# One core of a two-layer transformer: FP4 feed-forward products in split reduced precision, and small vector operations handed to POOL

## The chip, the cores and the metric

The program runs on one core of one Trainium2 chip. That core has a matrix engine (TensorE; PE is its matmuls and PEld its weight loads), VectorE (DVE), ScalarE (ACT), GpSimd (POOL) and a queue for transfers (SP). The metric is the device time of one execution in microseconds. Before the change it is 1334.26 us, the median of 3 runs (1334.25 to 1334.98).

## The reference

The input x has 8 sequences of 512 rows and 256 columns. Two layers follow, each of them x = x + attention(layernorm(x)), then x = x + ffn(layernorm(x)):

- Layer 0, attention: 16 heads of 16 columns, causal over all 512 positions, with gamma and beta on the normalized input and one weight for q, k and v.
- Layer 0, feed-forward: `h = silu(gate) * y`, hidden width 704, where every product is an "FP4 linear". Blocks of 16 values, of the weights and of the inputs alike (and of h), are scaled by their largest magnitude over 6 and rounded to the grid 0, 0.5, 1, 1.5, 2, 3, 4, 6. So the layer has three matrix products, and a rounding to the grid ahead of each.
- Layer 1, attention: the same heads, but a row sees only itself and the 63 before it; four weights and four biases.
- Layer 1, feed-forward: hidden width 768, weights that are integers from -127 to 127 over 127, no rounding of the inputs.

## The kernel before, in words

A sequence is one "batch" b of 8, held in SBUF as `X[b]`: 128 partitions by 4 row tiles t by 256 columns. The work goes through four stages: attention 0, FFN 0, attention 1, FFN 1.

**Attention** (function `attention`, used twice). A unit is a batch and half of the heads, a quad is four heads of a unit, so there are 32 quads per stage. Three ways of ordering matter. The PE work is written out by hand and pinned in program order (`pin`). All other instructions are put in order on their engines by a planner, which works with modelled costs; an engine then executes its own list strictly in that order. And `body` sets what is interleaved: while quad i makes its exponentials (`Outputs`), the scores of quad i+2 are formed only to find the row maxima (`scores`, whose `tensor_reduce` on DVE is L469 in attention 0 and L488 in attention 1). `maxima(i+2)` (L508) then splits each maximum into three bfloat16 pieces by two subtractions in a row on DVE, and `max_rows` (pm, L519) turns the pieces by a matmul into rows that enter the next product. It runs one quad later, at step 3 of 6 in attention 0 and at step 1 of 4 in attention 1. The exponentials come from ACT (L575, L605), POOL clears what the mask forbids (`only`, L134), and PE sums (`sums`, L635).

Beside this run the preparations for later batches. `row_stats` makes the layernorm statistics: DVE `bn_stats`, then ve (L161, L165) on DVE, the power -1/2 on POOL (rs, L166) and mr on DVE again (L168); `normalize` (L174) is on ACT. `load_q`, `load_k` and `stores` form q and k in three bfloat16 pieces (L374 to L378 on ACT and DVE, L387 and L390 on POOL), write them to HBM and fetch them back in another layout. In attention 0 a generator, `filler`, is advanced three times in ten steps: it rounds the FP4 weights (`quantize` with `exact`) and prepares the first batch of FFN 0.

**FFN 0** works on 32 tiles of 128 rows. `gated` (L1026) forms gate and up in two halves of 352 columns by 4-byte matmuls, whose records come two to a matmul. ACT takes silu (L1031) and DVE multiplies (L1032). `quantize` rounds h: a reduce (L217), the scale (L223), its reciprocal (L224), a correction of the reciprocal (L225), a product on POOL (L226), ACT (L274), two operations on DVE (L276, L278) and a product on POOL (L279). `down` transposes h on PE (L1041), copies it to SBUF in three pieces on ACT (L1045 to L1048), multiplies it by wd1 (L1052), and DVE adds it to X (L1056). It runs two tiles behind `gated`. `prepare` makes the inputs of the next batch in the same way, tagged x. Late in the stage the integer weights of layer 1 arrive and `opening` of attention 1 begins.

**FFN 1** already uses the type float32r, with a high and a low half of its inputs; one record is one matmul there (L1159, L1131).

## Time and profile before

| | |
|---|---|
| median of 3 runs | 1334.26 us |
| the profiled execution, its own time | 1330.82 us |
| its span on the core | 1329.1 us |
| mean granted TensorE clock | 0.98 |
| attention 0 with its start (0 to 486) | 486 us |
| FFN 0 (486 to 806) | 320 us |
| attention 1 (806 to 1165) | 359 us |
| FFN 1 (1165 to 1329) | 164 us |

The bounds of the stages are read from the first and last start of each line's instructions; the end of one and the beginning of the next overlap by a few us. A line of a group reads: line, engine, operation, output<-input, shapes, count | busy us, mean ns of one | idle time of the engine just before them, and who ended it. A line of a timeline reads: start, duration, engine, line, operation, count, and in brackets the idle time before it. A line of stages reads: start:end, length, then for each engine the busy us and the number of instructions, the granted clock, the share of the DMA engines and GB/s.

### The profile page before, as it was taken

The numbers are of one execution on the slowest core, as the hardware profiler recorded it, in microseconds if no ns is written. First come the engines' busy times: TensorE is split into PE (matmuls) and PEld (weight loads), VectorE is DVE, ScalarE is ACT, GpSimd is POOL, SyncE is SP. The second block draws the span as 40 slices with busy tenths as digits, with TensorE's granted clock in tenths as the row PEclk, the third lists the DMA queues.
The fourth block names the chain that finished last, engine by engine and source line by source line (L and its number), as shares of the span: only waits on it lengthen the run. The fifth ranks groups of instructions, "written<-read, shape, count | busy, mean of one in ns | idle before, by whom it ended". The sixth has DMA issues, their size and how long they took to land. (4 is left out here: it accounts for less than half of the span.)

```text
span 1329.1 us, 23108 instructions
## 1 busy us (share of the span) xinstructions
PE 1185.7 (89%) x8815; PEld 791.4 (60%) x8846; DVE 929.9 (70%) x1657; ACT 650.8 (49%) x1057; POOL 688.7 (52%) x912
## 2 busy tenths in 40 slices
PE   4678889889978998998999998999999999889998
PEld 2444454445534455665666666676767667668887
DVE  4699989796699847686766657676667767545553
ACT  3265655566665663332333323544455444555553
POOL 4266556464456334443443544766667566634443
PEclk9899999899989998999999999999999999999999
DMA  7643334354433310000000044454543535000001
GB/s 219 142 103 75 87 80 91 83 111 87 96 68 97 60 33 1 24 24 0 1 1 0 0 111 93 96 123 84 113 103 91 125 80 128 7 0 33 25 33 42
DMA packets 50448, 92.07 MB, mean 69 GB/s; under 512 B 6428, under 2 KB 43420, under 8 KB 44188
## 3 DMA queue, kind: packets, MB, share of 16 engines
q1 hardware_dynamic: 49452, 89.74, 29.6%
q8 instruction: 72, 1.18, 0.4%
q10 hardware_dynamic: 816, 0.79, 0.2%
q14 instruction: 44, 0.36, 0.1%
q0 software_dynamic: 64, 0.00, 0.0%
HBM read 61.15 MB, written 29.36 MB: 68 GB/s over the span
## 5 line engine op out<-in xcount | busy, mean ns | idle before, releaser
L134 POOL TENSOR_SCALAR_AFFINE_SELECT ex<-ex 128x256 f32<-128x256 f32 (+2 forms) x512 | 263.4, 525 | 230.3 <-ACT ex L575 129.9
L575 ACT ACTIVATE ex<-t 128x1024 f32<-128x1024 f32 (+1 forms) x192 | 168.0, 882 | 121.1 <-PE t L564 110.7
L469 DVE TENSOR_REDUCE mx<-s 128x2 f32<-128x1024 f32 (+2 forms) x192 | 196.6, 1035 | 39.9 <-PE s L458 30.6
L605 ACT ACTIVATE ex<-t 128x640 f32<-128x640 f32 (+1 forms) x128 | 96.8, 757 | 123.4 <-PE t L595 108.6
L635 PE MATMUL po<-ex,vp 128*32 128x128 f32 (+4 forms) x2816 | 142.9, 322 | 3.1 <-POOL ex L134 2.0
L488 DVE TENSOR_REDUCE mx<-s 128x4 f32<-128x768 f32 x128 | 121.3, 953 | 31.9 <-PE s L482 30.9
L1052 PE MATMUL pd<-wd,hT 128*128 128x256 f32 (+1 forms) x384 | 101.3, 407 | 15.9 <-ACT hT L1045 15.1
L635 PEld LDWEIGHTS po<-ex,vp 128*32 128x32 f32 x2816 | 71.2, 109 | 60.5 <-issue 31.2
L1103 POOL TENSOR_TENSOR hT<-gh,hT 128x512 fp32r<-128x512 f32 x48 | 61.7, 1291 | 82.6 <-ACT hT L1102 66.1
L453 PE MATMUL s<-kk_both,qq_both 96*128 96x512 bf16 (+3 forms) x352 | 81.9, 314 | 19.0 <-DVE mx L469 8.8
L1052 PEld LDWEIGHTS pd<-wd,hT 128*128 128x128 f32 (+1 forms) x384 | 70.1, 195 | 47.9 <-ACT hT L1045 28.0
L279 POOL TENSOR_TENSOR h<-mg_h,sc_h 128x704 f32<-128x704 bf16 x32 | 45.4, 1420 | 97.6 <-DVE mg_h L278 90.3
L1026 PE MATMUL gu<-wg,fyT 128*128 128x352 f32 x256 | 93.9, 470 | 0.0
L1026 PE MATMUL gu<-wu,fyT 128*128 128x352 f32 x256 | 86.3, 459 | 0.0
L475 PE MATMUL s<-wmask,ident_b 128*128 128x384 bf16 x256 | 83.6, 332 | 1.4 <-DVE mx L488 1.4
L564 PE MATMUL t<-qq_both,kk_both 108*128 108x512 bf16 (+3 forms) x352 | 70.4, 304 | 12.1 <-DVE mx L469 6.1
L226 POOL TENSOR_TENSOR xn_h<-h,rc_h 128x704 f32<-128x704 f32 x32 | 45.0, 1405 | 61.1 <-DVE rc_h L225 57.5
L458 PE MATMUL s<-cmask,ident_b 128*128 128x128 bf16 (+1 forms) x321 | 76.4, 238 | 0.0
L1170 DVE SCALAR_TENSOR_TENSOR gh<-ggu,gsl 128x512 f32<-128x512 f32 x48 | 33.2, 691 | 55.6 <-ACT gsl L1168 55.1
L1031 ACT ACTIVATE sl<-gu 128x352 f32<-128x352 f32 x64 | 29.4, 460 | 75.8 <-PE gu L1026 75.6
L1026 PEld LDWEIGHTS gu<-wu,fyT 128*128 128x128 f32 x256 | 48.6, 190 | 27.4 <-issue 1.0
L453 PEld LDWEIGHTS <-qq_both 96*128 96x128 bf16 x352 | 32.6, 101 | 51.5 <-issue 29.6
(256 smaller groups left out, 2661.1 us busy)
## 6 DMA issues: line engine op xcount, KB each, us to landing
q_hbm<-qp SPq DMA_DIRECT2D x96, 128.0 KB
k_hbm<-kp SPq DMA_DIRECT2D x96, 128.0 KB
qq_both<-q_hbm SPq DMA_DIRECT2D x44, 256.0 KB
kk_both<-k_hbm SPq DMA_DIRECT2D x22, 384.0 KB
qq_both<-q_hbm SPq DMA_DIRECT2D x44, 128.0 KB
kk_both<-k_hbm SPq DMA_DIRECT2D x22, 256.0 KB
qq<-q_hbm SPq DMA_DIRECT2D x20, 256.0 KB
out_dram<-go SPq DMA_DIRECT2D x16, 256.0 KB
```

What stands on the lines that cost most here:

```text
L134: nc.gpsimd.affine_select(out=t, in_=t, compare_op=ALU.is_ge, fill=0.0, base=base, pattern=[[0, n] for n in shape[1:-1]] + [[sign, shape[- ...
L453: pin(nc.tensor.matmul(bank[:, a * w : (a + 1) * w], lhsT=q[:KF, hs[j], t * P : w], rhs=k[:KF, hs[j], :w], start=(a == 0), stop=False, ski ...
L458: pin(nc.tensor.matmul(bank.rearrange("p (i k) -> p i k", k=w)[:, :, t * P :], lhsT=ident_b, rhs=cmask[:, : len(part), :], start=False, st ...
L469: nc.vector.tensor_reduce(dst, src, AX.X, ALU.max)
L475: pin(nc.tensor.matmul(sc[:, a, : 2 * BAND], lhsT=ident_b, rhs=mask.rearrange("p a k -> p (a k)"), start=True, stop=False,))
L488: nc.vector.tensor_reduce(mx[:, t2 : t2 + 2, js[0] : js[0] + 2].rearrange("p t j -> p j t"), sc[:, :, : 2 * BAND].rearrange("p j (t k) -> ...
L564: pin(nc.tensor.matmul(bank[:, a * w : (a + 1) * w], lhsT=k[: KF + 12, self.hs[j], t * P : (t + 1) * P], rhs=q[: KF + 12, self.hs[j], t * ...
L575: nc.scalar.activation(ex[:, :banks, :used], sc[:, :banks, :used], AF.Exp, scale=QSCALE)
L605: nc.scalar.activation(by_head[:, :, :w], sc[:, :, :w], AF.Exp, scale=QSCALE)
L635: pin(nc.tensor.matmul(self.o[HP * j : HP * (j + 1), t * P : t * P + w], lhsT=vp[:, kt, 4 * c + j, :], rhs=self.ex[kt, j][:, x0 : x0 + w], ...
L1026: nc.tensor.matmul(gu[:, i, :352], lhsT=YT[b][:, e, t * P : (t + 1) * P], rhs=w[:, e, f], start=(e == 0), stop=(e == NE - 1),)
L1052: nc.tensor.matmul(pd[:, :D], lhsT=hT[:n, k, :], rhs=wd1[:n, k, :], start=(k == 0), stop=(k == NH - 1),)
```

## The change

FFN 0: the 4-byte matmuls become three float32r matmuls each, high by high, high by low, low by high. The weights are split at the end of `filler` (wg, wu and the inputs of batch 0) and at the start of the stage (wd); every later input and h is split as it leaves PSUM (`split`: a copy on ACT, a subtraction on DVE). h is padded from 704 to 768 columns. The transposes of a tile (`turn_rows`) move ahead of `gated`, three tiles behind it, and `down` stays after it. `prepare` starts one tile earlier. `quantize` in its inexact form works in place, and its correction of the reciprocal is gone (the constant of the scale takes its place).

Attention: the two subtractions of `maxima` go from DVE to POOL. The statistics' operations after `bn_aggr` are all on POOL. Statistics are taken one quad before `normalize`, and `normalize` is spread over four steps. Masks are added by `minus_b` with the opposite sign. The second tile of values and `cmask` move into the pools of the stages, so the clearing of that tile on POOL happens at the start of each attention's body. The opening of attention 1 keeps its pieces of q and k in a shared tile and has one remainder buffer.

```diff
-        nc.vector.tensor_scalar(ve, mv[:, :, 1], EPS, None, ALU.add)
         if twice:
-            nc.vector.scalar_tensor_tensor(ve, ve, EPS, mv[:, :, 1], ALU.mult, ALU.add)
+            nc.gpsimd.tensor_scalar(ve, mv[:, :, 1], EPS, EPS, ALU.add, ALU.mult)
+            nc.gpsimd.tensor_tensor(ve, ve, mv[:, :, 1], ALU.add)
+        else:
+            nc.gpsimd.tensor_scalar(ve, mv[:, :, 1], EPS, None, ALU.add)
         nc.gpsimd.tensor_tensor(rs, ve, mhalf, ALU.pow)
         mr = small.tile([P, NT], F32, tag="mr", name=f"mr_{tag}")
-        nc.vector.scalar_tensor_tensor(mr, mv[:, :, 0], -1.0, rs, ALU.mult, ALU.mult)
+        nc.gpsimd.tensor_tensor(mr, mv[:, :, 0], rs, ALU.mult)
+        nc.gpsimd.tensor_scalar(mr, mr, -1.0, None, ALU.mult)
...
-            nc.vector.tensor_scalar(sc, am, sixth, 1e-12, ALU.mult, ALU.max)
+            nc.vector.tensor_scalar(sc, am, SIXTH_UP, 1e-12, ALU.mult, ALU.max)
             nc.vector.reciprocal(rc, sc)
-            nc.vector.tensor_scalar(rc, rc, DOWN, None, ALU.mult)
-            nc.gpsimd.tensor_tensor(blocks(xn), src, wide(rc), ALU.mult)
+            nc.gpsimd.tensor_tensor(src, src, wide(rc), ALU.mult)
...
+    PAIRS = ((0, 0), (0, 1), (1, 0))
+    def split(hi, lo, src):
+        nc.scalar.copy(hi, src)
+        nc.vector.tensor_tensor(lo, src, hi.bitcast(F32), ALU.subtract)
...
             for a in range(2):
-                nc.vector.tensor_tensor(
+                nc.gpsimd.tensor_tensor(
                     mx[:, :, a + 1, :], mx[:, :, a, :], upper(mx)[:, :, a, :], ALU.subtract
                 )
...
+            padded_values(home[0], 1, nc.gpsimd)
             norm(1)
...
+                if r == 0 and c + 2 < B:
+                    at(f3, lambda: stats(c + 2))
                 if r == 1 and c + 2 < B:
-                    at(f1, lambda: norm(c + 2))
+                    for t in range(NT):
+                        at(t, lambda t=t: norm(c + 2, [t]))
...
+        for t, nm, homes in (
+            (wg1, "wg", (high, high)), (wu1, "wu", (high, high)), (YT[0], "y", (wp, wp)),
+        ):
...
+            for e in range(NE):
+                nc.scalar.copy(hi[:, e], t[:, e])
+                nc.gpsimd.tensor_tensor(lo[:, e], t[:, e], hi[:, e].bitcast(F32), ALU.subtract)
+                yield
...
+        nc.scalar.copy(wd_halves[0], wd1)
+        nc.gpsimd.tensor_tensor(
+            wd_halves[1], wd1, wd_halves[0].bitcast(F32), ALU.subtract
+        )
...
-            for i, w in enumerate((wg1, wu1)):
+            for i, w in enumerate((HALVES["wg"], HALVES["wu"])):
+                n = 0
                 for e in range(NE):
-                    nc.tensor.matmul(
-                        gu[:, i, :352], lhsT=YT[b][:, e, t * P : (t + 1) * P],
-                        rhs=w[:, e, f], start=(e == 0), stop=(e == NE - 1),
-                    )
+                    for l, r in PAIRS:
+                        nc.tensor.matmul(
+                            gu[:, i, :352], lhsT=YT[b][l][:, e, t * P : (t + 1) * P],
+                            rhs=w[r][:, e, f], start=(n == 0), stop=(n == 3 * NE - 1),
+                        )
+                        n += 1
...
+        def turn_rows(b, t):
+            h = HID.pop((b, t))
+            hT = HT[b, t] = [
+                fp.tile([P, NH, P], F32R, tag=f"hT{i}", name=f"hT{i}_{b}_{t}", bufs=1)
+                for i in range(2)
+            ]
+            pt = psum2(f"ph_{b}_{t}").rearrange("p a k -> p (a k)")
+            for k in range(NH):
+                nc.tensor.transpose(
+                    pt[:, k * P : (k + 1) * P], h[:, k * P : (k + 1) * P], ident
+                )
+            flat = [x.rearrange("p k t -> p (k t)") for x in hT]
+            split(flat[0], flat[1], pt[:, : NH * P])
...
+            for l, r in PAIRS:
+                for k in range(NH):
+                    nc.tensor.matmul(
+                        pd[:, :D], lhsT=hT[l][:, k, :], rhs=wd_halves[r][:, k, :],
+                        start=(l == r == k == 0), stop=(l == 1 and k == NH - 1),
                     )
...
-        for n in range(len(tiles) + 2):
+        for n in range(len(tiles) + 3):
+            if n >= 3:
+                turn_rows(*tiles[n - 3])
...
-                if t == 0 and b + 1 < B:
-                    ahead = prepare(b + 1)
+                if n == 0:
+                    ahead = prepare(1)
+                    for _ in range(3):
+                        next(ahead)
+                elif t == NT - 1 and b + 2 < B:
+                    ahead = prepare(b + 2)
                 gated(b, t, 0)
                 gated(b, t, 1)
...
-            if n >= 2:
-                down(*tiles[n - 2])
+            if n >= 3:
+                down(*tiles[n - 3])
```

## The prediction

> **What bounds the kernel now.** I read the page's slices first, then the busy time of each engine by stage, then PE's timeline in the two feed-forward stages, and last the waits in the attentions. By stage:
>
> ```profile
> 66.00:300.00 234.00, 200.16 (x1507) 110.92 (x1522) 211.05 (x340) 139.92 (x197) 135.40 (x169) 0.98 0.42 90
> 300.00:366.00 66.00, 64.89 (x501) 35.44 (x505) 45.36 (x67) 43.16 (x63) 28.98 (x49) 1.00 0.43 90
> 366.00:465.00 99.00, 83.35 (x656) 45.06 (x663) 88.71 (x187) 61.25 (x86) 50.70 (x72) 0.95 0.35 75
> 529.40:761.50 232.10, 217.72 (x889) 145.55 (x887) 162.64 (x277) 83.23 (x189) 97.59 (x67) 0.99 0.03 7
> 835.00:1165.00 330.00, 306.22 (x3549) 225.12 (x3548) 222.84 (x398) 160.61 (x241) 220.37 (x387) 0.98 0.42 94
> ```
>
> The columns after the length are PE, PEld, DVE, ACT, POOL. Attention 0 is bound by DVE (211 of 234 us, 89 of 99) wherever the rounding of the weights runs beside it, and by PE (65 of 66) where it does not. FFN 0 (24 tiles here) is bound by PE: 218 of 232, with DVE at 163. Attention 1 is bound by PE with 24 us of gaps; POOL is 67% busy. FFN 1 fills PE.
>
> One FFN 0 tile on PE lasts 9.67 us (one gate-up-transposes-down round is 605.37 to 615.04 in the timeline):
>
> ```profile
> 610.27 0.76 PE L1026 MATMUL gu<-wg,fyT 128*128 128x352 f32 x2
> 612.06 3.05 PE L1052 MATMUL pd<-wd,hT 128*128 128x256 f32 x12 [1.03 <-ACT hT L1045]
> 615.04 0.86 PE L1026 MATMUL gu<-wg,fyT 128*128 128x352 f32 x2
> 616.92 1.35 PE L1026 MATMUL gu<-wg,fyT 128*128 128x352 f32 x4
> 618.10 1.35 PE L1026 MATMUL gu<-wu,fyT 128*128 128x352 f32 x4
> 619.29 0.82 PE L1041 MATMUL ph<-ident,h 128*128 128x128 f32 x6
> ```
>
> Starts count, not durations, since matmuls overlap. 616.92 to 618.10 is 1.18 us for four records, which are two 4-byte matmuls: 0.59 us each. 612.06 to 615.04 is 2.98 us for the six of `down`, with 1.03 us of waiting for ACT's copy ahead of them. FFN 1 shows what the new type costs:
>
> ```profile
> 1199.74 1.07 PE L1159 MATMUL ggu<-yT,wu_r 128*128 128x512 f32 x4
> 1200.65 1.59 PE L1131 MATMUL gpd<-wd_r,hT 128*128 128x256 f32 x12
> 1202.09 1.09 PE L1159 MATMUL ggu<-yT,wg_r 128*128 128x512 f32 x4
> ```
>
> Four of 512 columns start within 0.91 us (0.2275 each), twelve of 256 within 1.44 us (0.120 each). Between the two, 352 columns cost 0.160.
>
> **FFN 0, PE.** Removed: 8 gate and up matmuls x 0.59 = 4.72 us, `down` 2.98, the wait 1.03. Kept: six transposes 0.65 (619.29 to 619.94), two of the inputs at 0.1 each, 0.2. That is 9.58 of the 9.67. Added: 24 x 0.160 = 3.84 and 18 x 0.120 = 2.16; the wait should go, because the copies (ACT about 0.8, DVE 0.95) then lie under 3.84 us of gate and up. New PE time 3.84 + 2.16 + 0.65 + 0.2 = 6.85, with 0.35 for hand-overs 7.2 us.
>
> **FFN 0, DVE**, which is late next. The rows for 24 tiles:
>
> ```profile
> L278 DVE SCALAR_TENSOR_TENSOR mg_x<-mg_x,xn_x 128x1024 bf16<-128x1024 bf16 x6 | 10.7, 1792 | 0.0
> L225 DVE TENSOR_SCALAR rc_h<-rc_h 128x44 f32<-128x44 f32 x25 | 10.0, 398 | 0.6
> L276 DVE SCALAR_TENSOR_TENSOR xn_x<-mg_x,xn_x 128x1024 f32<-128x1024 bf16 x6 | 7.4, 1225 | 15.9 <-ACT mg_x L274 15.9
> L225 DVE TENSOR_SCALAR rc_x<-rc_x 128x64 f32<-128x64 f32 x6 | 7.0, 1165 | 0.0
> ```
>
> The correction L225 goes: 17.0 us. L278 writing 4-byte values in place should cost what L276 does: 3 us less for x, nothing for h (907 and 905 ns). Added: the low half of h, 24 times 768 columns out of PSUM. The same subtraction of 512 columns takes 685 ns (L1103), an addition of 256 takes 416 (L1056), so 0.95 us, 22.8 in all; and 12 low halves of inputs x 0.685 = 8.2. Sum 162.6 - 17.0 - 3 + 31.0 = 174 us, 7.25 us a tile against 6.78. So PE falls to 7.2 while DVE rises to 7.25: neither hides the other. Two engines that hand work to each other in fixed orders do not both reach 100%. DVE in attention 0 reaches 90%; at that share the tile takes 8.0 us. Ends: 7.3 (DVE full) and 9.0 (80%). Gain 32 x 1.67 = 53 us. ACT falls (one copy of 768, about 0.8, for three of 585, 274 and 264 ns) and POOL stays at 4.1 us a tile: both are covered at half load, and without that cover would have to double first.
>
> Splitting the weights: ACT four copies of 704 and two of 512 (about 4 us at 585 ns for 512), POOL four subtractions of 704 and two of 512 (4 x 1.39 + 2 x 1.16 = 7.9 us). They use six more steps of `filler`, about 20 of the stage's 372, and end around 465 us by where the inputs' transposes lie now (441 us). Then PE is the one that is full and DVE is at 35%: nothing. If `filler` ran past the end, up to 8 us. wd: ACT 1.5, POOL 2.7 us (1.93 for 1024, 1.5 ns per further element), needed only by the third round; POOL's products for the first tiles wait behind it: 2 us taken, 0 to 4. The transfers keep number and size; the integer weights land in wd's old place, in a stage where DMA is 3% busy. The tighter buffers of the opening make PE wait for at most a store now and then, spread over eight rounds: nothing, 3 us if uncovered. FFN 0 in all: -51 us.
>
> **Attention, the maxima.** 128 subtractions of 16 elements leave DVE. Their cost there is uneven:
>
> ```profile
> 211.84 0.17 DVE L508 TENSOR_TENSOR mx<-mx 128x16 f32<-128x16 f32 x1
> 230.72 1.12 DVE L508 TENSOR_TENSOR mx<-mx 128x16 f32<-128x16 f32 x1
> ```
>
> 0.17 us alone, 1.12 while POOL works; 24.0 us in attention 0, 16.2 in attention 1. On POOL no row shows them. A tensor_tensor there costs 728 ns for 256 elements and 1930 for 1024, so 352 for 16; the smallest mask operation (128 columns) takes 297, the power on 4 elements 1020. I take 0.35, between 0.3 and 1.0: 0.7 us per quad, 45 us in all, and POOL goes from 67% to about 75% busy in attention 1. Where the table of engine selection in the Trainium skill's GPSIMD Engine Reference (4.1) gives elementwise work to VectorE, with GpSimd about twice slower, it speaks against this; twice DVE's 325 ns would be 83 us of POOL instead of 45, still inside its gaps. The page SBUF — State Buffer ("The single rule") adds that the two engines take an exclusive port lock, so the 45 us could come back as stalls of DVE's two-input operations; by it attention 0 would gain nothing.
>
> What waits: `max_rows` on PE. In attention 1 the pieces were ready at 953.68 us and used at 957.80: 4.1 us of slack, during which POOL has casts, subtractions and masks without a gap (953.85 to 961.5). The two can stand behind one of these, 1.2 to 1.4 us, and still be in time.
>
> **Attention, the statistics.** Of 8 batches and four kinds, 3 DVE instructions (4 where `twice`) become 3 or 4 on POOL, 104 more there x 0.35 = 36 us, under 0.1 to 1.0 each. What DVE loses is not only their time but a wait, since it stands still until POOL's power is done:
>
> ```profile
> 966.54 0.17 DVE L161 TENSOR_SCALAR ve_c<-mv_c 128x4 f32<-128x4 f32 x1
> 967.85 0.16 DVE L168 SCALAR_TENSOR_TENSOR mr_c<-mv_c,rs_c 128x4 f32<-128x4 f32 x1 [1.14 <-POOL rs_c L166]
> 967.92 0.95 DVE L488 TENSOR_REDUCE mx<-s 128x4 f32<-128x768 f32 x1
> 968.79 0.74 DVE L378 SCALAR_TENSOR_TENSOR qr<-pq,qcol,qp 128x512 f32<-128x512 f32 x1
> ```
>
> ```profile
> PE pm L519 <- DVE qr L378: 12.5, 12, 1.4
> ```
>
> Behind mr_c stand a reduce and qr, and for qr's bank PE's pm waits: 12.5 us in attention 1. With the statistics a quad earlier I expect about 7 of these back, less 3 for masks that come later from a fuller POOL: -4 us (between -12 and +10).
>
> Attention 0: in the two DVE-bound stretches DVE loses some 19 us of maxima (13.8 of them in 66 to 300), some 7 of the statistics' 10.2 and 3 of waits: 29 us. PE has 49 us of gaps there. I take half, -15, because POOL's load rises from 56% to 66% and stretches what DVE keeps; ends 0 and -29. The 66 us bound by PE keep their time.
>
> **The rest**: clearing the values' tile (1.83 us on POOL) falls into 5.9 us in which POOL is idle before its first cast in attention 1, and into a POOL 23% busy at 33 to 66 us; the first statistics get a longer POOL chain (about +0.8); other signs of masks nothing; FFN 1 nothing, PE being full. Together +2.
>
> **Sum.** -51 - 4 - 15 + 2 = -68. The profiled execution took 1330.82 us (span 1329.1 and 1.7 around it), 3.4 less than the median; I set it against the median: 1334.26 - 68 = 1266.
>
> **Rivals.** *Both engines fit better*: 7.4 us a tile, 71 from FFN 0 after its start, 25 in attention 0, 8 in attention 1, the same +2: 1232. For it: three tiles of distance between h and its transposes. Against: DVE then at 98%. *DVE's order sets FFN 0*: one buffer for the transposed h means a late low half stops `down`, then the next transposes; at 9.0 us a tile 21 - 2 = 19, attention 0 gives 8, attention 1 nothing: 1309. *POOL too late for the maxima*, the slower side: the pieces stand behind masks that themselves wait for ACT (up to 3.7 us per wait). Once POOL lags by more than the slack of 4.1 us, every quad's pm waits; from 68 / 64 = 1.06 us of PE waiting per quad on, the gain is gone, at 1.5 us the time is 1334 - 68 + 96 = 1362. Against it: POOL has a third of attention 1 idle, most of it waiting for ACT, and the pieces are ready before the last mask. *The new matmuls cost twice that*: 24 x 0.32 + 18 x 0.24 + 1.2 = 13.2 us a tile, 113 us more in FFN 0, 1430 with the -17 elsewhere; FFN 1's rows speak against it, and I give it nothing.
>
> **How the numbers follow.** Forecast 45%; better fit 22%; DVE's order 18%; POOL too late 5%; 7% between forecast and DVE's order, 3% beyond the better fit. Range 1232 to 1308, from one outer case to the other. 0.2% is what a measurement here tells from no change. Faster 0.94, within 0.01, slower 0.05.
>
> **What will show it.** FFN 0: tile distance near 8.0 us, DVE about 90% busy, no L1052 wait on ACT, 24 records of 352 columns at 0.16 us. Attention 0: DVE's share down, L508's place on POOL near 0.35 us each. Attention 1: pm without waits for qr; po's waits for POOL up little. It is wrong if the subtractions take 1 us on POOL, if 352 columns cost over 0.2 us, or if PE waits in FFN 0 for the low halves.

## The result, and the profile after

The changed kernel takes 1324.74 us (1324.02 to 1325.49): a ratio of 0.9941 to the kernel before, with a 95% interval of 0.9917 to 0.9965 (the two medians alone give 0.9929). The profiled execution took 1324.02 us with a span of 1322.3. So 9.5 us came in by the medians where 68 were forecast, and the time lies above the range.

The four stages, from the first gate matmul, the last `down` matmul, the first gate matmul of FFN 1 and the end of the span (us):

| | attention 0 | FFN 0 | attention 1 | FFN 1 |
|---|---|---|---|---|
| before | 485.6 | 321.2 | 367.4 | 154.9 |
| after | 492.8 | 300.8 | 375.0 | 153.8 |
| difference | +7.2 | -20.4 | +7.6 | -1.1 |

The differences add up to 6.7 us and not to 9.5, because the profiled execution of the kernel before was 3.4 us faster than its median. FFN 0 gained less than half of what was expected, and both attentions lost. The stages of the changed kernel; columns as in the prediction: stretch, length, busy us and instructions of PE, PEld, DVE, ACT, POOL, granted clock, share of the DMA engines, GB/s.

```profile
66.00:300.00 234.00, 199.11 (x1436) 108.37 (x1450) 180.43 (x257) 131.19 (x183) 139.14 (x208) 0.92 0.38 81
300.00:366.00 66.00, 56.00 (x431) 30.98 (x432) 50.44 (x83) 40.17 (x58) 35.70 (x58) 0.92 0.50 105
366.00:465.00 99.00, 91.20 (x733) 50.76 (x741) 81.23 (x149) 72.00 (x105) 70.45 (x117) 1.00 0.35 76
493.00:793.00 300.00, 257.18 (x1657) 242.87 (x1657) 238.37 (x378) 111.08 (x189) 145.31 (x113) 0.93 0.11 28
823.00:1160.00 337.00, 310.56 (x3568) 228.16 (x3567) 207.88 (x333) 163.17 (x246) 234.90 (x466) 0.98 0.42 93
```

DVE did lose its work in attention 0: 211 us of the first 234 became 180. A part of that is work that had not been reached yet; over the whole of attention 0 DVE's busy time falls from 387.9 to 359.6 us and POOL's rises from 249.1 to 289.3. But PE is at 199 of 234 as before: no engine is near full in this stretch now, and no time was won. In FFN 0 neither PE (257 of 300) nor DVE (238) is full. And the granted clock fell from 0.98 to 0.92 in the first stretch and from 0.98 to 0.93 in FFN 0.

**Attention 0.** From the timeline of the changed kernel:

```profile
122.06 1.23 POOL L158 TENSOR_SCALAR ve_a<-mv_a 128x4 f32<-128x4 f32 x1
123.37 0.20 POOL L159 TENSOR_TENSOR ve_a<-ve_a,mv_a 128x4 f32<-128x4 f32 x1
123.65 1.05 POOL L162 TENSOR_TENSOR rs_a<-ve_a,mhalf 128x4 f32<-128x4 f32 x1
124.78 0.20 POOL L164 TENSOR_TENSOR mr_a<-mv_a,rs_a 128x4 f32<-128x4 f32 x1
125.06 0.23 POOL L165 TENSOR_SCALAR mr_a<-mr_a 128x4 f32<-128x4 f32 x1
125.33 0.60 ACT L171 ACTIVATE y<-x,mr_a,rs_a 128x256 f32<-128x256 f32 x1 [5.26 <-POOL mr_a L165]
125.83 1.00 ACT L591 ACTIVATE ex<-t 128x1024 f32<-128x1024 f32 x1
126.89 0.80 PE L580 MATMUL t<-qq,kk 108*128 108x384 bf16 x2 [5.18 <-ACT ex L591]
```

The statistics' chain on POOL begins at 122.06 and ends at 125.29; the last of `bn_aggr` was done at 120.95. ACT, whose next instruction in its list is `normalize`, stands still for 5.26 us, the exponentials stand behind it, and PE waits 5.18 us for these. From 124.2 on the clock is at one half for 6.8 us.

**Attention 1** repeats this on a smaller scale:

```profile
863.32 0.23 POOL L161 TENSOR_SCALAR ve_c<-mv_c 128x4 f32<-128x4 f32 x1
863.63 1.04 POOL L162 TENSOR_TENSOR rs_c<-ve_c,mhalf 128x4 f32<-128x4 f32 x1
865.30 0.60 ACT L171 ACTIVATE by<-x,mr_c,rs_c 128x256 f32<-128x256 f32 x1 [2.53 <-POOL mr_c L165]
865.80 0.67 ACT L393 ACTIVATE qp<-pq,qcol 128x512 bf16<-128x512 f32 x1
866.57 0.75 DVE L394 SCALAR_TENSOR_TENSOR qr<-pq,qcol,qp 128x512 f32<-128x512 f32 x1 [0.92 <-ACT qp L393]
867.38 0.38 PE L535 MATMUL pm<-minus_b,mx 128*12 128x128 bf16 x4 [1.94 <-DVE qr L394]
```

The power waits behind POOL's masks, `normalize` for the power, qp behind `normalize`, DVE's qr for qp, and PE's pm for qr's bank. Over the stage pm waits 17.4 us for qr, against 14.0 before: the wait that the forecast saw going has grown. The pieces of the maxima themselves are never late: no wait of pm for them exceeds 0.2 us. The clock adds to the wait for qr: it drops to one half at 868.3, 916.1, 963.9 and 1011.7 us, each time right after pm has waited 1.94 to 1.96 us.

**FFN 0.** A tile's pitch (first gate matmul to the next tile's) goes 6.6, 8.2, 11.1, 6.6 in batch 2, 6.6, 6.7, 11.0, 10.7 in batch 5: mean 8.80 us over tiles 4 to 28, against 9.54 before. Of these 24 tiles 9 run at PE's own time, 6.6 to 6.7 us; the others are stretched. The stage's first four tiles (30.7 us before, 31.5 after) and its last whole three (35.0 and 36.2) gained nothing. In a stretched tile:

```profile
573.95 2.32 DVE L274 SCALAR_TENSOR_TENSOR fy<-mg_x,fy 128x1024 f32<-128x1024 bf16 x1
576.41 1.93 POOL L275 TENSOR_TENSOR fy<-fy,sc_x 128x1024 f32<-128x1024 f32 x1 [1.22 <-DVE fy L274]
578.38 0.19 DVE L220 TENSOR_SCALAR sc_h<-am_h 128x44 f32<-128x44 f32 x1 [0.99 <-POOL fy L275]
578.40 0.66 PE L878 MATMUL pt_f<-ident,fy 128*128 128x128 f32 x4 [0.86 <-POOL fy L275]
579.85 1.84 POOL L222 TENSOR_TENSOR h<-h,rc_h 128x704 f32<-128x704 f32 x1 [1.50 <-DVE rc_h L221]
581.37 0.97 PE L1141 MATMUL pd<-wd_high,hT 128*128 128x256 f32 x6 [0.90 <-DVE hT L285]
583.09 0.55 PE L1130 MATMUL ph<-ident,h 128*128 128x128 f32 x3 [0.75 <-POOL h L275]
```

The next batch's inputs (fy) pass through the same engines, and PE stops three times. Its waits in the stage (total, times, longest):

```profile
PE ph L1130 <- POOL h L275: 11.6, 8, 2.5
PE pt_f L878 <- DVE fyT L285: 7.6, 4, 3.1
PE pd L1141 <- DVE hT L285: 7.5, 6, 3.0
PE pt_f L878 <- POOL fy L275: 6.8, 3, 5.0
PE pd L1141 <- ACT hT L284: 4.6, 6, 2.3
```

**The clock.** Around one wait of 2.48 us in FFN 0, by windows of 3.4 us; the granted clock is the third number from the end:

```profile
649.90:653.30 3.40, 0.92 (x9) 0.72 (x8) 2.94 (x3) 1.62 (x3) 2.04 (x2) 0.99 0.00 0
653.30:656.70 3.40, 2.78 (x13) 2.41 (x12) 3.18 (x7) 1.32 (x3) 0.82 (x1) 0.50 0.00 0
656.70:660.10 3.40, 3.40 (x14) 3.40 (x13) 1.75 (x3) 2.24 (x6) 2.37 (x2) 0.50 0.01 2
660.10:663.50 3.40, 3.40 (x28) 3.40 (x26) 2.45 (x4) 1.40 (x3) 0.00 (x0) 1.00 0.00 0
```

PE was busy for 0.92 of the first window, and two windows at half clock follow; gate matmuls start 0.29 us apart there and 0.16 apart from 660.24 on. Half of PE's busy time inside such windows is what the clock cost at most: 21.8 us in the kernel before, 51.7 after (attention 0 11.9 and 20.8, FFN 0 4.8 and 19.1, attention 1 5.1 and 10.1, FFN 1 0 and 1.7).

### The profile page after: what moved, and what is told of

It is laid out like the page before. It is cut to its first block, busy times and chain, and to the rows that moved or that the text cites. A ratio compares the mean times of both kernels' runs of the same rounds, so it can differ in the third digit from the quotient of the medians.

```text
span 1322.3 us, 24142 instructions
## 1 busy us (share of the span) xinstructions
PE 1154.8 (87%) x9263; PEld 841.9 (64%) x9294; DVE 895.7 (68%) x1462; ACT 652.6 (49%) x1000; POOL 762.5 (58%) x1158
## 3 DMA queue, kind: packets, MB, share of 16 engines
q8 instruction: 75, 1.23, 0.4%
## 5 line engine op out<-in xcount | busy, mean ns | idle before, releaser
L275 POOL TENSOR_TENSOR h<-h,sc_h 128x704 f32<-128x704 f32 x32 | 45.8, 1433 | 72.8 <-DVE h L274 72.8
L491 PE MATMUL s<-wmask,minus_b 128*128 128x384 bf16 x256 | 84.6, 336 | 2.2 <-DVE mx L504 2.2
L580 PE MATMUL t<-qq_both,kk_both 108*128 108x512 bf16 (+3 forms) x352 | 72.2, 310 | 13.1 <-DVE mx L485 6.5
L474 PE MATMUL s<-cmask,minus_b 128*128 128x128 bf16 (+1 forms) x321 | 77.8, 242 | 0.0
L222 POOL TENSOR_TENSOR h<-h,rc_h 128x704 f32<-128x704 f32 x32 | 48.5, 1516 | 50.2 <-DVE rc_h L221 41.9
L1141 PE MATMUL pd<-wd_high,hT 128*128 128x256 f32 x384 | 60.6, 296 | 12.1 <-DVE hT L285 7.5
L1111 PE MATMUL gu<-wg_wgh,fyT 128*128 128x352 f32 x224 | 69.1, 350 | 0.0
L1111 PE MATMUL gu<-wu_wuh,fyT 128*128 128x352 f32 x224 | 65.4, 334 | 0.0
L1141 PEld LDWEIGHTS pd<-wd_high,hT 128*128 128x128 f32 x384 | 53.4, 199 | 15.3 <-DVE hT L285 8.7
L1256 PE MATMUL ggu<-yT,wg_r 128*128 128x512 f32 x192 | 57.5, 412 | 1.2 <-ACT yT L1199 0.8
L498 PE MATMUL s<-kk_both,qq_both 96*128 96x128 bf16 (+1 forms) x352 | 57.0, 244 | 0.4 <-DMA kk_both<-k_hbm 0.4
```

The lines of the kernel that those rows point to most:

```text
L474: pin(nc.tensor.matmul(bank.rearrange("p (i k) -> p i k", k=w)[:, :, t * P :], lhsT=minus_b, rhs=cmask[:, : len(part), :], start=False, st ...
L491: pin(nc.tensor.matmul(sc[:, a, : 2 * BAND], lhsT=minus_b, rhs=mask.rearrange("p a k -> p (a k)"), start=True, stop=False,))
L580: pin(nc.tensor.matmul(bank[:, a * w : (a + 1) * w], lhsT=k[: KF + 12, self.hs[j], t * P : (t + 1) * P], rhs=q[: KF + 12, self.hs[j], t * ...
L1111: nc.tensor.matmul(gu[:, i, :352], lhsT=YT[b][l][:, e, t * P : (t + 1) * P], rhs=w[r][:, e, f], start=(n == 0), stop=(n == 3 * NE - 1),)
L1141: nc.tensor.matmul(pd[:, :D], lhsT=hT[l][:, k, :], rhs=wd_halves[r][:, k, :], start=(l == r == k == 0), stop=(l == 1 and k == NH - 1),)
```

## The experiments

"Stages" gives attention 0, FFN 0, attention 1. The kernel before took 1331.8 to 1334.3 us beside these runs (medians); ratios are to that. A stage is read from one profiled execution and varies more than the median of a kernel: e2, e5 and e6, which differ in FFN 0 alone, have 498.7, 492.5 and 491.1 us in attention 0, while e7, e9, e11, e15 and e16, which run one and the same order there, have 485.4 to 487.2. So a stage that differs by a few us shows little unless the whole times go with it.

### The two moves undone, one by one and together

e1, on the changed kernel:

```diff
-                nc.gpsimd.tensor_tensor(
+                nc.vector.tensor_tensor(
                     mx[:, :, a + 1, :], mx[:, :, a, :], upper(mx)[:, :, a, :], ALU.subtract
```

> The changed kernel with the two subtractions of the maxima back on DVE, all else kept. Queue theory (what POOL and ACT wait for in their queues costs the attentions more than DVE's relief gives): POOL no longer stands still for DVE's maxima (32 us in the changed kernel), time 1312 to 1320. Relief theory (as predicted, the freed DVE time is worth half of itself in attention 0): DVE gets 40 us back, 1332 to 1345.

1329.54 us, 0.997 [0.9956, 0.9985]; stages 499.4, 296.6, 374.8.

e2, on the changed kernel (e3 is e1 and e2 together):

```diff
-            nc.gpsimd.tensor_scalar(ve, mv[:, :, 1], EPS, EPS, ALU.add, ALU.mult)
-            nc.gpsimd.tensor_tensor(ve, ve, mv[:, :, 1], ALU.add)
...
+        nc.vector.tensor_scalar(ve, mv[:, :, 1], EPS, None, ALU.add)
+            nc.vector.scalar_tensor_tensor(ve, ve, EPS, mv[:, :, 1], ALU.mult, ALU.add)
...
-        nc.gpsimd.tensor_tensor(mr, mv[:, :, 0], rs, ALU.mult)
-        nc.gpsimd.tensor_scalar(mr, mr, -1.0, None, ALU.mult)
+        nc.vector.scalar_tensor_tensor(mr, mv[:, :, 0], -1.0, rs, ALU.mult, ALU.mult)
```

> The changed kernel with ve and mr of the statistics back on DVE, all else kept. Queue theory: ACT's wait for mr in attention 1 falls from 21 us to below 10, PE's wait for pm's bank from 17 to about 12, time 1314 to 1321. Relief theory: DVE waits for POOL's power again, 1328 to 1336.

1316.41 us, 0.9866 [0.985, 0.9883]; stages 498.7, 297.8, 364.8.

> Both back on DVE. Queue theory: the sum of the two, 1303 to 1316. Relief theory: 1335 to 1355. If the two moves hardly matter: within 4 us of 1324.7, and the missing gain is all in FFN 0 and in the clock.

1324.59 us, 0.9927 [0.9906, 0.9947]; stages 498.1, 300.8, 365.9.

What follows: with the statistics taken early, attention 1 is 365 to 366 us with their operations on DVE and 375 with them on POOL, wherever the maxima are: 10 us. Undone together, the two moves cancel in the whole time (1324.59 against 1324.74 us). In attention 0 undoing them brings nothing back: it is at 498 us without either move, so its loss lies elsewhere too.

### Attention 0: which part of the change costs it

e7 is e3 without early statistics and without the spread `normalize`; e11 is e3 without early statistics alone:

```diff
-                if r == 0 and c + 2 < B:
-                    at(f3, lambda: stats(c + 2))
...
-                    for t in range(NT):
-                        at(t, lambda t=t: norm(c + 2, [t]))
+                    at(f1, lambda: norm(c + 2))
```

> On e3_both_on_dve (1324.59 us, attention 0 498.1 us against 485.6 before): the statistics are no longer taken a quad early and normalize is again issued in one step. If this order of issue is what costs attention 0 its 12 us, it goes back to 486 to 489 us and the whole to 1311 to 1316 us; attention 1 then has its waits of before again, 365 to 368 us. If it is not (the rest of the change, or where the half-clock windows fall), attention 0 stays at 494 to 502 us and the whole at 1320 to 1329 us.

1310.89 us, 0.9853 [0.9815, 0.9891]; stages 487.2, 299.7, 366.6. Up to quad 24 every quad starts within 1.2 us of where it started in the kernel before, so splitting the weights costs attention 0 next to nothing, as the forecast had it.

> On e7_norm_as_before (1310.89 us, attention 0 487.2 us): normalize is spread over four steps again, but the statistics are still taken when it begins; e3_both_on_dve, with the statistics a quad early as well, had 498.1 us in attention 0. If the spreading costs the 11 us, attention 0 is at 495 to 500 us and the whole at 1318 to 1326 us; if taking the statistics early does, attention 0 is at 486 to 489 us and the whole at 1309 to 1314 us.

1311.16 us, 0.9844 [0.9818, 0.9871]; stages 487.0, 299.4, 367.2. The spreading costs nothing (the instructions of DVE, ACT and POOL come in the same order in attention 0 as in e7); taking the statistics a quad early, with their operations on DVE, costs attention 0 the 11 us.

e8 is the kernel before with the two moves alone (both edits of e1 and e2, reversed):

> The kernel before with only the two moves of the change's name: the statistics' small operations and the two subtractions of the maxima on POOL, everything else as it was (statistics taken when normalize is issued). Relief theory (half of the DVE time freed in attention 0 returns, pm's waits for qr go): 1311 to 1322 us. Queue theory (a longer chain on POOL behind masks, ACT's normalize waits for it, and gaps over half a clock window drop the clock): within 5 us of 1334.3 or slower, 1330 to 1346 us.

1342.59 us, 1.0083 [1.0054, 1.0112]; stages 498.9, 318.7, 372.2. The two moves alone make the kernel before slower by 0.8%; attention 0 is 13.3 us longer. They did not come back as slower work on DVE: of its instructions in attention 0, those that both kernels have take 1.2 us more in all, in 389 us.

e10 is e7 with the maxima on POOL:

> On e7_norm_as_before (1310.89 us; attention 0 487.2, attention 1 366.6 us): of the attention's changes only the maxima's subtractions are on POOL. Relief theory (13.8 us less on VectorE in the stretch of attention 0 that it bounds, half of it returned): attention 0 478 to 483 us, in all 1302 to 1307 us. Queue theory (what VectorE gains is lost where a maximum's pieces stand behind casts and masks on POOL, and in half-clock windows): attention 0 486 to 495 us, in all 1309 to 1319 us.

1309.01 us, 0.9826 [0.98, 0.9853]; stages 482.7, 299.0, 369.6. Against e7 the maxima on POOL gain 1.9 us in all, 4.5 in attention 0, and attention 1 is 3.0 longer.

e18 is the changed kernel without early statistics (the first two lines of the diff of e7):

> The changed kernel (1324.74 us, attention 0 492.8, attention 1 375.0 us) with the statistics taken when normalize begins, not a quad earlier; their operations and the maxima stay on POOL. If the early place is what disturbs attention 0 (11 us with the operations on VectorE): attention 0 480 to 486 us; attention 1 then waits longer for the chain on POOL, 375 to 380 us; in all 1312 to 1322 us. If the early place costs only with the operations on VectorE: attention 0 489 to 497 us, in all 1321 to 1334 us.

1323.54 us, 0.993 [0.9908, 0.9952]; stages 501.2, 301.3, 368.4. Attention 0 came out above both expectations, and attention 1 did not wait longer, against the first: only the early place and POOL together cost it its time. From e10 the kernel differs by the statistics' operations on POOL (and by the spreading, which cost nothing in e11), and attention 0 is 18.5 us longer, the whole 14.5. This pair shows best that relief is not time.

The four kernels with the maxima on POOL, whole time, then attention 0 and 1 (us):

| | statistics' operations on DVE | on POOL |
|---|---|---|
| taken with `normalize` | e10: 1309.0; 482.7, 369.6 | e18: 1323.5; 501.2, 368.4 |
| taken a quad early | e2: 1316.4; 498.7, 364.8 | changed kernel: 1324.7; 492.8, 375.0 |

Each of the two, the early place and POOL, lengthens attention 0 by itself, and they do not add up. In the changed kernel as it is, POOL's 8.3 us (against e2) lie in attention 1. To the pair of the first row: from e10, and then from e18, the stretch 66 to 465 and ACT's wait for the statistics in 60 to 480:

```profile
66.00:465.00 399.00, 351.77 (x2679) 194.43 (x2707) 329.97 (x536) 249.40 (x354) 240.83 (x356) 0.96 0.40 84
...
ACT y L168 <- DVE mr_a L162: 10.6, 5, 6.4
```

```profile
66.00:465.00 399.00, 346.44 (x2565) 188.93 (x2568) 308.34 (x483) 236.22 (x335) 235.83 (x374) 0.93 0.40 84
...
ACT y L171 <- POOL mr_a L165: 24.8, 6, 9.2
```

DVE is busy 21.6 us less in the same 399 us, but PE does fewer instructions too (2565 for 2679): over the whole of attention 0 DVE is freed of 8.6 us (368.9 and 360.3). `normalize` waits 14.2 us longer, for a chain that stands between POOL's masks and casts; and what the half clock costs PE there rises from 14.3 to 22.1 us at most. The same wait of ACT is 11.6 us in the kernel before, 23.2 in the changed one, 24.8 in e8, 22.5 in e1, 11.9 in e2, 15.0 in e3 and 11.7 in e11. Among the kernels without early statistics (before, e10, e11 against e8, e18) attention 0 is long where this wait is; among those with them it is not so: e2 has 11.9 us of it and 498.7 us, the changed kernel 23.2 and 492.8. So the wait goes with the loss only where the statistics are taken late; that it is the cause there is argued from the timeline above, and no run separates it from the planner's new order. With the statistics on POOL an earlier place helps attention 0 (501.2 to 492.8); with them on DVE it hurts (487.0 to 498.1), where this wait explains 3 us at most.

One thing that goes with the losses is a wait of DVE of 6.7 to 7.4 us for the second half of the up weights, whose transfer is issued near 235 us behind stores of k, near 200 in the kernel before. e13 and e14 issue it earlier:

```diff
+        def rounded(n, *args):
+            for i, _ in enumerate(quantize(*args)):
+                if i == 4:
+                    load(n + 1)
+                yield
...
```

> The changed kernel (1324.74 us, attention 0 492.8 us) with the transfer of the next part of the weights issued at the fifth step of the part before it, where it was issued when its own rounding begins. If the transfer's place behind the stores of k is what costs attention 0 its time (7.0 us of VectorE standing for it, and the rounding of the up weights some 50 us later than in the kernel before): no such wait, attention 0 480 to 487 us, in all 1311 to 1319 us. If the wait only goes with another cause (gaps over half a clock window): attention 0 489 to 497 us, in all 1320 to 1330 us.

1322.07 us, 0.9902 [0.9865, 0.9939]; stages 490.0, 302.4, 375.0. That wait is gone.

> The same edit on e12_own_buffers_maxima (1305.01 us, attention 0 481.0 us). If the place of the transfer is the cause: attention 0 474 to 479 us, in all 1297 to 1303 us; if not, 1303 to 1311 us.

1311.18 us, 0.9841 [0.982, 0.9863]; stages 488.3, 296.0, 366.8, slower than e12 below. So the late transfer is not the cause; e10 has that wait too (6.8 us), and is the shorter in attention 0 (482.7 us). Why the early place costs attention 0 time with the operations on DVE stays open. PE's loss to the clock there is 22.9 us at most in e3 against 13.1 in e11, which goes with the loss but was not separated from it.

### FFN 0: what stretches the tiles

e4, on the changed kernel:

```diff
-            hT = HT[b, t] = [
-                fp.tile([P, NH, P], F32R, tag=f"hT{i}", name=f"hT{i}_{b}_{t}", bufs=1)
-                for i in range(2)
-            ]
+            one = fp.tile([P, NH, P], F32R, tag="hT0", name=f"hT0_{b}_{t}", bufs=1)
+            hT = HT[b, t] = [one, one]
...
-            split(flat[0], flat[1], pt[:, : NH * P])
+            nc.scalar.copy(hT[0].rearrange("p k t -> p (k t)"), pt[:, : NH * P])
```

> The changed kernel without the low half of h: its subtraction on DVE (0.95 us a tile) is left out, and down's third product takes the high half again, so PE's work is the same. If DVE's load sets FFN 0: tiles fall by about 1 us, 25 to 32 us in all, 1293 to 1300. If the wait for the next batch's inputs and the clock that falls in its gaps set it: tiles without prepare stay at 6.6, the others lose little, 1312 to 1322.

1323.84 us, 0.9909 [0.9882, 0.9936]; FFN 0 301.5, mean tile 8.71 us. The first line is e4, the second the changed kernel:

```profile
530.00:710.00 180.00, 152.67 (x1043) 149.56 (x1042) 139.21 (x209) 68.69 (x120) 86.47 (x55) 0.95 0.03 10
```

```profile
530.00:710.00 180.00, 156.36 (x1038) 151.15 (x1038) 153.22 (x232) 70.09 (x121) 84.35 (x54) 0.93 0.03 10
```

DVE falls from 85% to 77%, and the tiles are as long as they were. So neither a late low half of h nor DVE's mean load sets the pitch. DVE's load where it is bunched is another matter. The four tiles of batch 5 in the changed kernel, and the third of these in e4:

```profile
664.20:670.80 6.60, 6.60 (x51) 6.60 (x49) 5.46 (x11) 2.39 (x4) 4.27 (x3) 1.00 0.01 4
670.80:677.50 6.70, 6.70 (x52) 6.69 (x50) 6.27 (x7) 2.70 (x5) 1.39 (x1) 1.00 0.00 0
677.50:688.50 11.00, 8.33 (x55) 7.67 (x53) 10.42 (x15) 3.45 (x6) 6.06 (x4) 0.95 0.00 0
688.50:699.20 10.70, 9.14 (x54) 8.76 (x53) 7.78 (x13) 4.96 (x9) 3.26 (x3) 0.73 0.01 2
```

```profile
684.80:695.30 10.50, 8.64 (x58) 8.40 (x57) 9.77 (x15) 3.84 (x7) 6.22 (x5) 0.90 0.00 1
```

In the first stretched tile DVE is busy for 10.42 of 11.0 us, and in e4 still for 9.77 of 10.5, although the mean fell; in the second (7.78 of 10.7) it is not full, and the clock is at 0.73.

e5, on e2:

```diff
+        rows.append(wp.tile([P, NH * P], F32, tag="fyT", name="h4"))
...
-            if n >= 3:
-                turn_rows(*tiles[n - 3])
+            if n >= 4:
+                turn_rows(*tiles[n - 4])
...
-            if n >= 3:
-                down(*tiles[n - 3])
+            if n >= 4:
+                down(*tiles[n - 4])
```

> The statistics' operations are back on VectorE (as in e2_stats_on_dve, 1316.41 us, FFN 0 297.8 us), and the transposes of a tile and its down product come four tiles behind its gate instead of three, with a fifth buffer for the rows of h. Distance theory: PE's waits for POOL's last product of h (11.1 us in 7 waits there) go, and with them some of the half-clock windows (41 us in that stage); the waits of the next batch's inputs (11.7 us) and of the transposed h (12.8 us) stay: FFN 0 280 to 292 us, in all 1300 to 1311 us. Queue theory in its strict form (the tiles in which the next batch is prepared are limited by what stands in the in-order queues, so a longer distance only shifts the wait): FFN 0 stays within 4 us, 1312 to 1321 us.

1313.18 us, 0.9869 [0.9835, 0.9903]; FFN 0 296.3, mean tile 8.74. The wait of ph for POOL is gone, and the waits for the inputs have taken its place:

```profile
PE pt_f L875 <- DVE fyT L282: 15.7, 5, 3.9
PE pd L1139 <- DVE hT L282: 9.3, 8, 3.0
```

e6, on e2:

```diff
-                            gu[:, i, :352], lhsT=YT[b][l][:, e, t * P : (t + 1) * P],
+                            gu[:, i, :352], lhsT=YT[min(b, 1)][l][:, e, t * P : (t + 1) * P],
...
-                elif t == NT - 1 and b + 2 < B:
+                elif False:
```

> On e2_stats_on_dve (1316.41 us, tile 8.71 us). Leaves out part of the computation: the inputs of batches 2 to 7 of FFN 0 are not prepared, all these batches use those of batch 1. If the preparation is what stretches two of four tiles to 10 to 12 us, every tile goes to 6.6 to 7.2 us and the half-clock windows of FFN 0 go too: 24 tiles by 1.5 to 2.1 us is 36 to 50 us, 1266 to 1282 us. If the stretched tiles come from the rounding of h and its order on VectorE and POOL, the mean stays above 8.0 us: over 1298 us.

1276.81 us, 0.9586 [0.9552, 0.962]; FFN 0 261.8. Where nothing else runs, every tile takes 6.6 us, and the mean over tiles 4 to 28 is 7.25; the longer ones lie in batches 2 to 4, where the weights of layer 1 are prepared. The transposes of three tiles in a row:

```profile
681.80 0.82 PE L1127 MATMUL ph<-ident,h 128*128 128x128 f32 x6
688.44 0.82 PE L1127 MATMUL ph<-ident,h 128*128 128x128 f32 x6
695.07 0.82 PE L1127 MATMUL ph<-ident,h 128*128 128x128 f32 x6
```

So the preparation of six batches costs 36.0 us. e15 and e16 leave out its halves, both on e7:

```diff
+        if b < 2:
             yield from quantize(pool, blocks, blocks, P, 64, f"x{b}", False)
+        else:
+            for _ in range(4):
+                yield
```

> On e7_norm_as_before (1310.89 us, FFN 0 299.7 us). Leaves out part of the computation: the inputs of batches 2 to 7 of FFN 0 are normalized, transposed and split, but not rounded to the grid (6 us of VectorE, 4 of POOL, 1 of ACT per batch). If the rounding stretches the two tiles of four: mean tile 6.9 to 7.5 us, FFN 0 262 to 272 us, in all 1273 to 1284 us. If the transposes with their copies do, mean tile over 8.2 us, in all over 1298 us.

1285.55 us, 0.9649 [0.9628, 0.967]; FFN 0 269.9, mean tile 7.63.

> On e7_norm_as_before (1310.89 us, FFN 0 299.7 us). Leaves out part of the computation: the inputs of batches 2 to 7 of FFN 0 are normalized and rounded, but not transposed and split; these batches use the inputs of batch 1. If the rounding stretches the tiles: mean tile over 8.2 us, in all over 1298 us. If PE's wait for the rounded inputs and for the bank's release (11 to 16 us by name in this stage) does, mean tile 6.9 to 7.5 us, in all 1273 to 1284 us. Both may share it: then both runs stand between.

1308.80 us, 0.9824 [0.9804, 0.9845]; FFN 0 297.3, mean tile 8.52. Its largest wait in the stage:

```profile
PE ph L1128 <- POOL h L272: 18.2, 9, 3.8
```

By the stage the rounding of the inputs costs 29.8 us and the transposes 2.4 (by the mean tile 28 and 7; one of the last tiles of e16 took 22 us). Without the transposes PE waits for h instead.

e9, on e7, gives that rounding its own small buffers:

```diff
...
+            own_x[f"x{b}"] = wp.tile([P, 1024], F32, tag="fyT", name=f"own_{b}")
             y = normed(fp, "y", b)
```

> On e7_norm_as_before (1310.89 us; FFN 0 299.7 us, mean tile 8.80 us). The rounding of the next batch's inputs gets its own four small tiles (am, sc, rc, mg), where it shared two of each with the rounding of h. Buffer theory (the inputs hold one of two buffers for some 20 us, so that the scale of the next h stands on VectorE until POOL's product is done: 5.2 us of that wait by name in the changed kernel, and everything behind it): the two stretched tiles of four lose 1 to 2 us each, FFN 0 280 to 292 us, in all 1291 to 1303 us. Bunching theory (VectorE has 8.8 to 11.6 us of work in these tiles whatever the buffers are): FFN 0 within 4 us of 299.7, in all 1307 to 1315 us.

1307.53 us, 0.9816 [0.9788, 0.9845]; FFN 0 297.6. The wait of sc_h for POOL's fy (5.2 us in 7) is gone, and 2 us are won. e12 is e9 with the maxima on POOL:

> The inputs' own buffers of e9_own_buffers_x and the maxima on POOL of e10_maxima_on_pool_only together, on e7_norm_as_before (1310.89 us). If both theories that promise a gain hold: 1283 to 1300 us. If neither does, within 6 us of 1311 us.

1305.01 us, 0.9804 [0.9775, 0.9832]; stages 481.0, 296.2, 367.1. It is the fastest complete kernel of this study.

e17, on e12, issues the rounding in quarters:

```diff
+            runs = [
+                quantize(pool, y[:, t].rearrange("p (n k) -> p n k", k=16),
+                         y[:, t].rearrange("p (n k) -> p n k", k=16), P, 16, f"x{b}", False, t)
+                for t in range(NT)
+            ]
...
```

> On e12_own_buffers_maxima (1305.01 us, FFN 0 296.2 us, mean tile 8.61 us): the rounding of the next inputs is issued as four instructions of 256 columns for each one of 1024, with the same work. If its long instructions (1.2 to 1.9 us on VectorE, 1.3 to 1.9 on POOL) hold up the chain of h behind them in the in-order queues: FFN 0 280 to 290 us, in all 1289 to 1299 us. If the work as such counts, the additional fixed costs of some 21 instructions a batch make it the same or slower: FFN 0 295 to 303 us, in all 1304 to 1312 us.

1307.14 us, 0.9792 [0.9771, 0.9814]; FFN 0 297.5. Shorter instructions do not help. Both e9 and e17 came out where they were expected if the work as such counts, on VectorE above all, whatever its buffers and the length of its instructions.

## Why the prediction was wrong, step by step

By the stages the forecast missed by 30.6 us in FFN 0 (51 expected, 20.4 measured), by 22.2 in attention 0 (15 to be gained, 7.2 lost) and by 11.6 in attention 1 (4 to be gained, 7.6 lost).

**FFN 0, PE: right.** A tile without a stretch takes 6.6 us, where 6.85 and 0.35 of hand-overs were forecast; the records of 352 columns start 0.16 us apart, those of 256 columns 0.12. The waits for the copies of h went in these tiles; the stretched ones kept them, so over the stage pd's fell only from 15.9 to 12.1 us. The rival of doubled matmul costs fell, and so did the better fit.

**FFN 0, DVE: the sizes were near, the step from load to time failed.** The low half of h takes 942 ns (forecast 0.95) and that of the inputs 682 (0.685). The last operation on the inputs, which "should cost what L276 does", 1225 ns, takes more; the group in the changed kernel:

```profile
L274 DVE SCALAR_TENSOR_TENSOR fy<-mg_x,fy 128x1024 f32<-128x1024 bf16 x7 | 13.5, 1927 | 0.0
```

DVE is at 85%, not 90. But the step that took 8.0 us from a DVE at 90% treated DVE's work as spread evenly and its mean load as what sets the pitch. e4 took the low halves of h away and gained nothing. e6 and e15 show what stretches the tiles: the preparation of the next inputs, 36.0 us, and in it their rounding, 29.8. That the old pitch of 9.5 us had room for it is argued: no run leaves it out of the kernel before. The step "32 x 1.67" also counted all tiles at the steady pitch: the 24 steady ones gained 0.74 us each, 17.9 in all, and the other eight with the stage's end 2.5. The tile was 8.80 us, inside the ends 7.3 and 9.0, and the stage gained 20.4 us, near the rival's 19; but that rival's mechanism, the late low half, fell with e4, although its sign showed (PE waits 15.1 us for the low halves in the two L285 rows). That the tile fell inside its ends and the stage near a rival is luck. The rounding costs about 5 us a batch (29.8 / 6), nearly all of DVE's work for it (5 to 6 us). So what fits best is DVE's work bunched in one or two tiles of four, where it is nearly full (10.42 of 11.0 us) while it has a seventh of its time free on average; but the second stretched tile does not show it, and no run spread this work over four tiles. More distance (e5), own buffers (e9) and shorter instructions (e17) each moved the wait and won 2 us of the stage at most.

**Attention, the maxima: right in sign.** On POOL a subtraction takes 268 ns, below the 0.35 taken:

```profile
L524 POOL TENSOR_TENSOR mx<-mx 128x16 f32<-128x16 f32 x124 | 33.3, 268 | 14.5 <-DVE mx L485 10.2 <-DVE mx L504 3.2
```

In four pairs of kernels that differ in this move alone it gains 1.9 us (e7 to e10), 2.5 (e9 to e12), 4.8 (e1 to the changed kernel) and 8.2 (e3 to e2) of the whole time, and pm waits for them for at most 0.2 us: the rival "POOL too late for the maxima" fell. The 3.0 us that e10 loses in attention 1 do not repeat from e9 to e12 (368.4 and 367.1). The GPSIMD Engine Reference of the Trainium skill (4.1), which the prediction weighed, puts GpSimd at about twice VectorE's time for such operations; here the same 124 subtractions took 330 ns each on DVE in the kernel before and 268 on POOL (medians of all 128: 176 and 215). The prediction's other doubt, that POOL's work comes back as stalls of DVE's two-input operations, did not come true either, as the 1.2 us of e8 show; attention 0 gained nothing, but not for that.

**Attention, the statistics: the step that failed most.** The text named who waited for whom on DVE, and wrote that DVE loses "a wait, since it stands still until POOL's power is done". It did not ask who waits for the finished chain: ACT's `normalize`, with exponentials and qp behind it. On POOL the chain stands between masks and casts that themselves wait for ACT. The price per instruction was not the error (means of 200 to 540 ns, of the power 1.04 to 1.33 us). Attention 1 was to gain 4 and lost 7.6; with the operations back on DVE (e2) it gains 2.6, with the late place (e18) it loses 1.0. Attention 0 was to gain 15 by half of what DVE was freed of; it lost 7.2. By e18 against e10 the operations' place costs it 18.5 where the statistics are taken late; in the changed kernel, where they are early, moving the operations back does not help it (e2). "I take half" had no mechanism behind it: DVE was freed of 28 us over attention 0, near the 29 that the text expected, and none came back.

**The early statistics were not costed as a step of their own**, only as help for attention 1. By e3 against e11 they cost attention 0 11 us with the operations on DVE; by which path stays open.

The steps add up in this order: 1334.26 before; about 1311 with everything but the two moves and the early statistics (e11); 1309.0 with the maxima on POOL (e10); 1323.5 with the statistics on POOL (e18); 1324.7 with them taken early. The product in float32r is the gain, the statistics on POOL give 14.5 us of it back in this order (8.3 with the early place, by e2), and the two moves by themselves (e8) lose.

**The clock was left out.** It stood in the stage rows (0.95 to 1.00), but every gain and loss was counted at full speed. The loss to it rose by 30 us at most, in a forecast that missed by 59. The Trainium skill's page "TensorE: Matmul & The Clock Gate" (section "Why this matters for your kernels") advises to leave no idle gaps above about 3 us; by that rule the waits of 1.7 to 2.5 us here are harmless, and the runs do not bear it out, as the last section shows.

## What to carry to other kernels

Before moving a small operation to a less busy engine, follow its result: name the instruction that consumes it, what stands in that engine's list behind the consumer, and what stands on the new engine ahead of the operation; that price can exceed all the time the old engine is freed of. When a change takes a third off the engine that bounds a loop, look for the work that comes once in several rounds, because it may no longer fit in the slack that hid it, and cost it by a run without it. A wait of PE of 2 us may cost twice its length where it drops the clock: by the rows above, half of at least one window of 3.4 us comes on top, an estimate.

## What was not expected of the hardware

The granted clock changes on a fixed grid of 3.413 us. From 60 us on, it drops to one half in the changed kernel after windows in which PE was idle for 1.52 to 2.95 us, and does not after up to 1.70; in the kernel before it drops after 1.74 to 3.41 and does not after up to 1.89. So about half a window of idling is enough, in one piece or several, and whether a wait of 2 us does it depends on where the grid lies. At half clock a matmul of 352 columns takes 0.29 us for 0.16. The clock comes back after a window in which PE was idle for at most 0.6 us. The changed kernel falls into it 24 times before its end, the kernel before 10 times.

POOL's times for small operations depend on the work beside them: ve_a takes between 0.19 and 1.23 us, a subtraction of the maxima between 0.21 and 1.23. In the changed kernel 14 of the 128 subtractions took 0.38 us or more, the others at most 0.30. Each of the 14 began while DVE worked on inputs from SBUF, and ended 0.07 to 0.08 us after DVE did:

```profile
412.10 1.22 DVE L274 SCALAR_TENSOR_TENSOR fy<-mg_x,fy 128x1024 f32<-128x1024 bf16 x1
412.17 1.23 POOL L524 TENSOR_TENSOR mx<-mx 128x16 f32<-128x16 f32 x1
```

Those that began beside nothing but DVE's reduces of the scores (25) or its subtractions out of PSUM (L391, 10) were not stretched.
